# Where the input sums of a seven-product matrix multiplication are formed in a two-layer attention kernel

## The chip, the cores and the metric

The kernel runs on one core of one Trainium2 chip. The metric is device microseconds of one execution. The engines are named as the profile names them: PE is TensorE (matrix products; PEld its weight loads), DVE is VectorE, ACT is ScalarE, POOL is GpSimd and SP is SyncE. [...]

## What is computed

The reference, cut to what matters; there are two such layers, one after the other:

```python
# x: (16, 256, 32, 32); b = 16 images, c = 256 channels, n = 32*32 = 1024 positions
def layer(x, Wq, bq, Wk, bk, Wv, bv, rel_h, rel_w):        # 4 heads of d = 64
    y = _gn(x)                       # (y - mean) / sqrt(var + 1e-5) in 16 groups of the last axis
    xf = y.reshape(b, c, n)
    q, k, v = (einsum('oc,bcn->bon', W, xf) + bias[None, :, None] for W, bias in ...)
    sim  = einsum('bhdi,bhdj->bhij', q, k)
    rel  = (rel_h + rel_w).reshape(heads, d, n)
    qpos = einsum('hdi,bhdj->bhij', rel, q)
    attn = softmax(sim + qpos, axis=-1)
    out  = einsum('bhdn,bhmn->bhdm', v, attn)
    return x + out.reshape(b, c, w, h)
```

All numbers are float32.

## The kernel before

The work is cut into 32 units, one for each image and layer. Their order is written out by hand in the list `units`, so that an image's second layer comes some units after its first. A unit has four blocks, b = 0 to 3: two pairs of heads (`pr`) times two halves of the 1024 query positions (`half`). A block works on a score matrix of both heads of the pair against 8 groups of 128 key positions, j = 0 to 7, each held in a tile of 128x1024 in two PSUM banks. There are four such pairs of banks, and the list `ring` says which of them is used for what.

For each j, `seed` (L447, VectorE) writes the position term into PSUM, `scores` (L483, TensorE) adds the product of q and k, ScalarE takes the exponential into a tile p (L492), and `add_up` (L522, L524, VectorE) adds p to the block's running sum acc. `attend` (L537, TensorE) multiplies the p of all j with the values. The last one or two p of a block are added to acc in the next block, by adding transfers from POOL (`add_last`, L555); a p buffer comes free only when they have landed. The sums over the partitions are folded by more transfers: `fold` (L560, POOL), `stack_up` (L574, SP), `fold_again` (L579, POOL), `fold_stack` (L584, POOL, several times with falling sizes) and `spread_sums` (L592, SP), which writes them into den_all. One and a half units of blocks later `reciprocals` takes 1/den_all on VectorE (L634), writes it to DRAM (rd, L636, SP) and reads it back spread over the partitions (rden, two transfers, L641, SP). `normalise` (L649, VectorE) multiplies the block's output od by it, and `add_by_dma` (L667, POOL) adds that to the image x.

In every block other work stands between the scores: the next unit's projections (`project`, L268; `positions`, L424, which ScalarE copies out at L435), its norm, and its values. The norm of unit u + 2 is computed by sums and squares on ScalarE (L190), a small product on TensorE, and in `norm_var` a reduction on VectorE (L235) followed on POOL by the power -0.5 (L237) and the shift (L239, tile nshift). `norm_apply` (L248, ScalarE) writes the normalised image xn, in pieces spread over blocks 0 and 1.

The order of instructions on each engine is the order in which the code calls them; nothing reorders them. An engine that waits holds all that stands behind it in its own queue.

The values of unit u + 1 are computed in block 3 (`block_with_values`) by the seven-product scheme for a 2x2 block matrix multiplication. The class `Values` has the seven products: numbers 1, 2 and 3 read quarters of xn, and number 3's weights are a mixture; numbers 4, 5, 6 and 7 read t, a tile of four quarters of 128x512 that are sums of quarters of xn. With the quarters called x0 to x3,

- t0 = x1 + x0, t1 = x1 + x3
- t2 = t0 + x3, t3 = t2 + x2

The products go through two banks, in four pairs of stages called "1" to "4", with copies by ScalarE (`keep`, L404) and additions by VectorE (`combine`, L410) between. Stage "2" holds products 6 (which reads t2) and 2 and is the first to read t; "3" reads t0 and t1, "4" reads t3.

Before the change t is formed in block 2 by transfers alone: SP copies x1 twice (`sum_copies`, L327), POOL adds x0 and x3 to the two copies (`sum_additions`, L336), SP copies t0 twice, POOL adds x3 to both, and at block 2's end POOL adds x2 to the last quarter.

Of the kernel before, what the change touches and what calls it, by code (L numbers as in the profile page):

```python
# [13 lines left out]
ALU = mybir.AluOpType  # L14
# [3 lines left out]
P = 128  # L18
HALF = 512
# [33 lines left out]
def fast_path(ctx, tc, sh, x, layers, out, W, den_all, good, flag):  # L53
# [26 lines left out]
    nc = tc.nc  # L80
# [234 lines left out]
    sums_x = {}  # L315

    def quarters_of_x(u):
        return xns[u].rearrange("p c (a n) -> p (c a) n", a=2)

    def sum_copies(u, second):  # L320

        x = quarters_of_x(u)
        if not second:
            sums_x[u] = tpool.tile([P, 4, HALF], F32, tag="t", name=f"t_{u}")
        t = sums_x[u]
        into, of = (t[:, 2:4, :], t[:, 0:1, :]) if second else (t[:, 0:2, :], x[:, 1:2, :])
        nc.sync.dma_start(into, of.to_broadcast([P, 2, HALF]))  # L327

    def sum_additions(u, i):
        x, t = quarters_of_x(u), sums_x[u]  # L330
        into, of = (
            (t[:, 0:2, :], x[:, 0:4:3, :]),
            (t[:, 2:4, :], x[:, 3:4, :].to_broadcast([P, 2, HALF])),
            (t[:, 3, :], x[:, 2, :]),
        )[i]
        nc.gpsimd.dma_start(into, of, accum_op=ALU.add)  # L336

    def by_token(bank):
        return bank.rearrange("p (i c) -> p i c", c=P)
# [102 lines left out]
    def seed(blk, j, tag):  # L442

        u, pr, half = blk
        ps = psum2(tag, f"ps_{u}_{pr}_{half}_{j}")
        ab = abt[u, pr][:, :, j, :]
        nc.vector.tensor_tensor(  # L447
            ps.rearrange("p h (w y) -> p h w y", y=H),
            ab[:, :, :H].unsqueeze(2).to_broadcast([P, 2, XH, H]),
            ab[:, :, H + half * XH : H + (half + 1) * XH]  # L450
            .unsqueeze(3)
            .to_broadcast([P, 2, XH, H]),
            ALU.add,
        )
        seeds[blk, j] = ps
# [60 lines left out]
    def add_up(blk, j):  # L516
        u, pr, half = blk
        if j == 0:
            return
        if j == 1:  # L520
            accs[blk] = apool.tile([P, 2, HALF], F32, tag="acc", name=f"acc_{u}_{pr}_{half}")
            nc.vector.tensor_tensor(accs[blk], probs[blk, 0], probs[blk, 1], ALU.add)  # L522
        else:
            nc.vector.tensor_tensor(accs[blk], accs[blk], probs[blk, j], ALU.add)  # L524
# [102 lines left out]
    def reciprocals(u, pr, count=2):  # L627

        n = index[u, pr, 0]
        r8 = fpool.tile([P, 2, 8], F32, tag="r8", name=f"r8_{u}_{pr}")
        nc.vector.reciprocal(r8[:, :count, :], den_all[:, n : n + count, :])  # L634
        rd = dpool.tile([P, count * 8], F32, tag=f"rd{count}", name=f"rd_{u}_{pr}")
        nc.sync.dma_start(rd, r8[:, :count, :].rearrange("p x e -> p (x e)"))  # L636
        rden = opool.tile([P, 2 * HALF], F32, tag="rden", name=f"rden_{u}_{pr}")
        rdens[u, pr] = rden
        rd = rd.rearrange("(h k) e -> h (k e)", h=2)
        for h, hs in enumerate(QUARTERS):  # L640
            nc.sync.dma_start(  # L641
                rden[hs, : count * HALF],
                rd[h : h + 1].to_broadcast([D, count * HALF]),
            )
# [117 lines left out]
    def block(n):  # L762
        blk = blocks[n]
        u, b = divmod(n, BPU)
        pr_, half = blk[1:]

        stacked = blocks[n - 3][:2] if half == 1 and n > 2 else None
        summed = blocks[n - 4][:2] if half == 0 and n > 3 else None
        last_unit = u + 1 == NU
        before = blocks[n - 5][:2] if b == 1 and n > 4 else None  # L770
        after = blocks[n + 1] if n + 1 < len(blocks) else None
        previous = blocks[n - 1] if n > 0 else None
        one, two = u + 1 < NU, u + 2 < NU

        pieces = u + 1 < NU or b < 2
        if u + 1 == NU and b == 1:
            widen(u, 1)
        f0, f1, f2, f3 = ring
        folded = n - 1 < FOLDED
        if not pieces:  # L780
            return block_without_pieces(n, half)
        if b == 0 and u > 0:
            return block_with_q(n)
        if b == 3:
            return block_with_values(n)

        if b == 2:
            sum_copies(u + 1, False)
        if previous and folded and b == 1:
            add_last(previous, NT - 2)  # L790
        elif previous:
            add_up(previous, 6)
            if folded:
                add_last(previous)
            else:
                add_up(previous, 7)
        for j in range(1 if n > 0 else 2, 4):
            scores(blk, j)
        (first, first_out), (second, second_out) = prepare(u, b)
        first(0)  # L800
        norms(u, b, 0)
        if n == 1:
            reduced(2, 1)
            added(2)
        seed(blk, 4, f1)
        scores(blk, 4)
        add_up(blk, 1)
        if before:
            reciprocals(*before)
        norms(u, b, 1)  # L810
        second(0)
        if half == 1:
            second_out()
        if b == 2:
            sum_additions(u + 1, 0)
            sum_copies(u + 1, True)
        if stacked:
            fold_stack(*stacked, D)
        if summed:
            fold_stack(*summed, R // 8)  # L820
            spread_sums(*summed)
        if previous and folded:
            fold(previous)
        if stacked:
            fold_stack(*stacked, R)
        if b == 2:
            sum_additions(u + 1, 1)
        first(1)
        first_out()
        seed(blk, 5, f0)  # L830
        scores(blk, 5)
        if previous and folded:
            stack_up(previous)
        if b == 2 and n > 5:
            store(*blocks[n - 6][:2])
        add_up(blk, 2)
        if n == 0:
            reduced(2, 0)
        if half == 0:
            second(1)  # L840
            second_out()
        seed(blk, 6, f1)
        scores(blk, 6)
        if half == 0:
            ring[2:] = f3, f2
        seed(blk, 7, ring[2])
        scores(blk, 7)
        add_up(blk, 3)
        add_up(blk, 4)

        if after:
            seed(after, 0, f0)
        if n in check:
            next(checks)
        norms(u, b, 2)
        po = psum2(ring[3], f"po_{n}")
        values_of_p = attend(blk, po)
        values_of_p(0)
        if two and half == 1:
            mean_out = norm_mean(u + 2, filled(f1, f"pm_{n}", 0.0))  # L860
        if after:
            scores(after, 0)
        if n == 0:
            mean_out = norm_var(1, filled(f1, f"pm_{n}", EPS / 2))
        if stacked:
            fold_stack(*stacked, R // 2)
        if previous and folded:
            fold_again(previous)
        if b == 2:
            sum_additions(u + 1, 2)  # L870
        if half == 1 and u + 3 < NU and units[u + 3][1] == 0 and u > 0 or n == 3:
            load_x(units[u + 3][0], range(pr_, pr_ + 1) if u > 0 else range(CC))
        add_up(blk, 5)
        if n in (2, 6):
            W.mix(n // 4)
        if before and last_unit:
            finish(*before)
        elif before:
            normalise(*before)
            add_by_dma(*before)  # L880
        if two and half == 1 or n == 0:
            mean_out()
        if stacked:
            fold_stack(*stacked, R // 4)
            if n == len(blocks) - 3:
                fold_stack(*stacked, R // 8)
                spread_sums(*stacked)
        if after:
            for j in range(1, 4):
                seed(after, j, ring[j % 3])  # L890
        norms(u, b, 3)
        values_of_p(1)
        take_out(blk, po)
        pos[n] = po
# [55 lines left out]
    def block_with_values(n):  # L950

        blk = blocks[n]
        u = blk[0]
# [6 lines left out]
        add_last(previous, NT - 2)  # L960
        scores(blk, 1)
        add_up(blk, 1)
        if before:
            reciprocals(*before)
        one = v.half(1, HI, False), v.half(1, LO, True)
        two_halves = score_half(blk, 2, 0), score_half(blk, 2, 1)
        v.stage("1", (two_halves[0], two_halves[1]), (one[0], one[1]), 0)
# [11 lines left out]
        v.keep(1, 0, 1.0)  # L979
        seed(blk, 5, r2)  # L980
        scores(blk, 5)
        seed(blk, 6, r1)
        scores(blk, 6)
        v.combine(0, 0, ALU.add)
# [24 lines left out]
        scores(after, 0)  # L1009
        v.pair("4", 3, 4, 1)  # L1010
        v.keep(0, 1, -1.0)
        fold_stack(*stacked, R // 2)
        fold_again(previous)
        if u + 3 < NU and units[u + 3][1] == 0:
            load_x(units[u + 3][0], range(1, 2) if u > 0 else range(CC))
        add_up(blk, 4)
        if two:
            mean_out()
        ring[:] = r1, r0, r3, r2
        seed(after, 1, r0)  # L1020
        if before:
# [526 lines left out]
```

## Time and profile before

| | |
|---|---|
| time, median of 3 runs | 2975.96 us (2975.19 to 2991.6) |
| profiled execution | 2993.0 us, span of its instructions 2989.0 us |
| PE busy | 2645.2 us (88%) |
| DVE busy | 2162.0 us (72%) |
| ACT busy | 2014.6 us (67%) |
| POOL busy | 1044.8 us (35%) |
| mean granted clock of TensorE | 0.946 |
| moved by DMA | 375.48 MB |

Busy times are shares of the whole span. Idle time in front of an instruction is shown in the profile beside what released it ("<-"): where TensorE is the engine that sets the pace, its own idle times and their releasers are the lines to read, and the other engines' idle times matter only where TensorE waits for them. The granted clock is the share of full speed at which TensorE was allowed to run. A unit of four blocks takes some 93 us, and most of what the trace shows repeats from unit to unit.

### The profile page before, as it was taken

How to read it: one execution, taken by the hardware profiler on the slowest of the kernel's cores; microseconds unless marked ns; L12 is line 12 of the kernel's file. 1: busy time of each engine (PE TensorE's matmuls, PEld its weight loads, DVE VectorE, ACT ScalarE, POOL GpSimd, SP SyncE). 2: the span in 40 equal slices, each digit the busy share in tenths (PEclk: the TensorE clock that was granted, in tenths of full speed). 3: DMA queues.
4: the chain of work that ended last, by engine and by line, in shares of the span. 5: the costliest groups of instructions: out<-in, count | busy, mean ns of one | idle time of the engine just before them, and what ended most of it. 6: DMA issues, size and time to landing. Idle time of an engine off the chain costs nothing. (4 is left out here: it accounts for less than half of the span.)

```text
span 2989.0 us, 94281 instructions
## 1 busy us (share of the span) xinstructions
PE 2645.2 (88%) x41192; PEld 1458.4 (49%) x41192; DVE 2162.0 (72%) x2091; ACT 2014.6 (67%) x3977; POOL 1044.8 (35%) x1122
## 2 busy tenths in 40 slices
PE   8988989888988889888899888988889888999897
PEld 4555544444445544454545544444454444444453
DVE  7877777666776767767777666776777767777777
ACT  7866776667766667666777666766677666776654
POOL 1334333333333433334343333333433334333330
PEclk9999999999989999999999999999999889999999
DMA  3666665667666666666766666566676556665663
GB/s 103 121 116 130 135 121 107 124 143 143 119 117 145 130 126 121 120 131 131 147 126 130 125 119 133 119 124 131 134 150 132 111 116 127 140 122 105 125 137 87
DMA packets 180099, 375.48 MB, mean 126 GB/s; under 512 B 58840, under 2 KB 60376, under 8 KB 179680
## 3 DMA queue, kind: packets, MB, share of 16 engines
q0 software_dynamic: 97072, 250.97, 48.4%
q1 hardware_dynamic: 82608, 118.41, 13.4%
q8 instruction: 326, 5.34, 0.7%
q14 instruction: 93, 0.76, 0.1%
HBM read 51.78 MB, written 17.30 MB: 23 GB/s over the span
## 5 line engine op out<-in xcount | busy, mean ns | idle before, releaser
L492 ACT ACTIVATE p<-ps,shift 128x1024 f32<-128x1024 f32 x993 | 1069.7, 1112 | 650.0 <-PE ps L483 570.5
L447 DVE TENSOR_TENSOR ps<-abt 128x1024 f32<-128x1024 f32 x1018 | 1225.6, 1227 | 331.2 <-ACT p L492 279.5
L483 PE MATMUL ps<-q,k 64*64 64x512 f32 x7944 | 1029.6, 612 | 100.8 <-DVE ps L447 96.6
L537 PE MATMUL po<-p,v 64*64 64x256 f32 x16384 | 973.5, 386 | 29.2 <-ACT q L279 27.1
L537 PEld LDWEIGHTS po<-p,v 64*64 64x64 f32 x16384 | 650.9, 137 | 377.0 <-issue 79.6
L524 DVE TENSOR_TENSOR acc<-acc,p 128x1024 f32<-128x1024 f32 x550 | 670.0, 1218 | 3.8
L483 PEld LDWEIGHTS ps<-q,k 64*64 64x64 f32 x7944 | 296.2, 137 | 516.5 <-DVE ps L447 249.9
L555 POOL DMA_DIRECT2D acc<-p x217 | 266.3, 1227 | 605.3 <-DMA acc<-p 241.4
L584 POOL DMA_DIRECT2D stack<-stack x310 | 308.8, 996 | 273.4 <-DMA stack<-stack 237.0
L368 PE MATMUL pw<-mixed,t 64*64 64x128 f32 x2976 | 172.7, 306 | 193.5 <-DMA t<-xn 193.5
L579 POOL DMA_DIRECT2D stack<-acc x248 | 215.6, 980 | 325.3 <-DMA stack<-acc 287.0
L248 ACT ACTIVATE xn<-x,nshift,rstd 128x128 f32<-128x128 f32 x496 | 209.1, 493 | 122.2 <-POOL nshift L239 122.2
L368 PEld LDWEIGHTS pw<-mixed,t 64*64 64x64 f32 x2976 | 151.6, 155 | 232.3 <-issue 208.8
L268 PE MATMUL pq<-xn,Wq 64*64 64x512 f32 x2048 | 243.0, 590 | 0.0
L268 PE MATMUL pk<-xn,Wk 64*64 64x512 f32 x2048 | 242.5, 589 | 0.0
L560 POOL DMA_DIRECT2D acc<-acc x124 | 102.0, 823 | 399.9 <-DMA acc<-p 389.5
L410 DVE TENSOR_TENSOR v<-v,pw 128x512 f32<-128x512 f32 x93 | 63.9, 687 | 240.9 <-ACT v L404 240.9
L522 DVE TENSOR_TENSOR acc<-p,p 128x1024 f32<-128x1024 f32 x128 | 156.4, 1222 | 93.9 <-ACT p L492 90.8
L336 POOL DMA_DIRECT2D t<-xn x93 | 130.2, 1400 | 249.3 <-DMA t<-t 195.8
L190 ACT ACTIVATE junk<-x,neg 128x128 f32<-128x128 f32 x505 | 197.7, 399 | 0.0
L368 PE MATMUL pw<-Wv,xn 64*64 64x128 f32 x1984 | 173.1, 326 | 0.2 <-issue 0.2
L368 PEld LDWEIGHTS pw<-Wv,xn 64*64 64x64 f32 x1984 | 148.4, 167 | 45.6 <-issue 45.4
(95 smaller groups left out, 1902.2 us busy)
## 6 DMA issues: line engine op xcount, KB each, us to landing
acc<-p POOLq DMA_DIRECT2D x217, 512.0 KB, 6.7
rden<-rd SPq DMA_DIRECT2D x126, 256.0 KB, 5.3
acc<-acc POOLq DMA_DIRECT2D x124, 256.0 KB, 3.6
t<-xn POOLq DMA_DIRECT2D x62, 512.0 KB, 6.9
x<-od POOLq DMA_DIRECT2D x61, 512.0 KB, 5.2
x<-in_x_dram SPq DMA_DIRECT2D x32, 512.0 KB, 4.3
stack<-acc SPq DMA_DIRECT2D x248, 64.0 KB, 2.1
stack<-acc POOLq DMA_DIRECT2D x248, 64.0 KB, 3.2
```

The lines of the kernel that those rows point to most:

```text
L190: nc.scalar.activation(junk, grouped(xt[units[u][0]], g), func, accum_out=into[:, g : g + 1], **bias)
L248: nc.scalar.activation(grouped(xns[u], g), grouped(xt[units[u][0]], g), AF.Identity, bias=shift[:, g : g + 1], scale=rstd[:, g : g + 1],)
L268: yield nc.tensor.matmul(pk[c, nh, :], w[l][rs, cc, c0 : c0 + D], xns[u][rs, cc, nh * HALF : (nh + 1) * HALF], start=(t == 0 and cc == 0), ...
L368: yield nc.tensor.matmul(self.pw[c, a, part * P : (part + 1) * P], x[rs, j0 : j0 + D], w[rs, :], start=first and not whole and part == 0, ...
L447: nc.vector.tensor_tensor(ps.rearrange("p h (w y) -> p h w y", y=H), ab[:, :, :H].unsqueeze(2).to_broadcast([P, 2, XH, H]), ab[:, :, H + h ...
L483: nc.tensor.matmul(ps[c, h, :], a[hs, j0 : j0 + D], b[hs, columns], start=bool(tag) and i == 0, stop=i == len(terms) - 1, skip_group_check ...
L492: nc.scalar.activation(p, ps, AF.Exp, bias=W.shift)
L524: nc.vector.tensor_tensor(accs[blk], accs[blk], probs[blk, j], ALU.add)
L537: yield nc.tensor.matmul(po[c, a, :QUART], vts[u][rs, pr, j, h * D : (h + 1) * D], p[rs, h, a * QUART : (a + 1) * QUART], start=(t == 0 an ...
L555: nc.gpsimd.dma_start(accs[blk], probs[blk, j], accum_op=ALU.add)
L579: nc.gpsimd.dma_start(at, acc[R:D, h, :], accum_op=ALU.add)
L584: nc.gpsimd.dma_start(stack[:rows_], stack[rows_ : 2 * rows_], accum_op=ALU.add)
```

## The change

t is formed by VectorE in three operations instead of two copies and three adding transfers. The first writes t0 and t1 together, the second t2, the third t3. They are issued in block 2: the first behind the additions of the previous block's last p, the second behind `add_up` 2, the third behind `add_up` 3.

Two other steps change places. `reciprocals` goes, in block 1, from behind `add_up` 1 to behind `add_up` 2, which is one seed and one addition later on VectorE; in block 3 it goes from behind `add_up` 1 to behind the scores of j = 5, two seeds later. And in block 3 `add_up` 4 and `mean_out`, which holds the reduction on VectorE and the power and the shift on POOL, go ahead of `fold_stack` with R // 2, `fold_again` and the load of x.

```diff
-    def sum_copies(u, second):
+    def add_inputs(u, i):
         x = quarters_of_x(u)
-        if not second:
+        if i == 0:
             sums_x[u] = tpool.tile([P, 4, HALF], F32, tag="t", name=f"t_{u}")
         t = sums_x[u]
-        into, of = (t[:, 2:4, :], t[:, 0:1, :]) if second else (t[:, 0:2, :], x[:, 1:2, :])
-        nc.sync.dma_start(into, of.to_broadcast([P, 2, HALF]))
-
-    def sum_additions(u, i):
-        x, t = quarters_of_x(u), sums_x[u]
-        into, of = (
-            (t[:, 0:2, :], x[:, 0:4:3, :]),
-            (t[:, 2:4, :], x[:, 3:4, :].to_broadcast([P, 2, HALF])),
-            (t[:, 3, :], x[:, 2, :]),
+        into, one, other = (
+            (t[:, 0:2, :], x[:, 0:4:3, :], x[:, 1:2, :].to_broadcast([P, 2, HALF])),
+            (t[:, 2, :], t[:, 0, :], x[:, 3, :]),
+            (t[:, 3, :], t[:, 2, :], x[:, 2, :]),
         )[i]
-        nc.gpsimd.dma_start(into, of, accum_op=ALU.add)
+        nc.vector.tensor_tensor(into, one, other, ALU.add)
...
 # block (b = 1 and b = 2)
-        if b == 2:
-            sum_copies(u + 1, False)
...
             else:
                 add_up(previous, 7)
+        if b == 2:
+            add_inputs(u + 1, 0)
...
         add_up(blk, 1)
-        if before:
-            reciprocals(*before)
...
-        if b == 2:
-            sum_additions(u + 1, 0)
-            sum_copies(u + 1, True)
...
-        if b == 2:
-            sum_additions(u + 1, 1)
...
         add_up(blk, 2)
+        if before:
+            reciprocals(*before)
+        if b == 2:
+            add_inputs(u + 1, 1)
...
         add_up(blk, 3)
+        if b == 2:
+            add_inputs(u + 1, 2)
         add_up(blk, 4)
...
-        if b == 2:
-            sum_additions(u + 1, 2)
...
 # block_with_values (b = 3)
         add_up(blk, 1)
-        if before:
-            reciprocals(*before)
...
         seed(blk, 5, r2)
         scores(blk, 5)
+        if before:
+            reciprocals(*before)
...
+        add_up(blk, 4)
+        if two:
+            mean_out()
         fold_stack(*stacked, R // 2)
         fold_again(previous)
         if u + 3 < NU and units[u + 3][1] == 0:
             load_x(units[u + 3][0], range(1, 2) if u > 0 else range(CC))
-        add_up(blk, 4)
-        if two:
-            mean_out()
```

## The prediction

> **What bounds the kernel now.** I read the page's busy shares first, then the list of waits, then TensorE's timeline around its longest wait, then the windows with the granted clock, and last GpSimd's queue.
>
> ```profile
> PE 2645.2 (88%) x41192; PEld 1458.4 (49%) x41192; DVE 2162.0 (72%) x2091; ACT 2014.6 (67%) x3977; POOL 1044.8 (35%) x1122
> ...
> L368 PE MATMUL pw<-mixed,t 64*64 64x128 f32 x2976 | 172.7, 306 | 193.5 <-DMA t<-xn 193.5
> ```
>
> TensorE is the fullest engine, yet idle for 2989.0 - 2645.2 = 344 us. More than half of that, 193.5 us, lies ahead of one group: the products that read the tile t of input sums. The list of waits gives the number of times and the next waits of TensorE:
>
> ```profile
> PE pw L368 <- DMA t<-xn: 193.5, 30, 10.8
> PE ps L483 <- DVE ps L447: 96.6, 67, 5.3
> PE po L537 <- ACT q L279: 27.1, 30, 1.2
> ```
>
> So in 30 of the 31 blocks with values, stage "2" waits 193.5 / 30 = 6.45 us for an adding transfer into t. TensorE's timeline in the unit near 1570 us (us from the start, duration, engine, line, operation, in brackets the idle time before):
>
> ```profile
> 1563.75 1.18 PE L424 MATMUL pa<-rel,q 64*64 64x64 f32 x64
> 1569.93 0.48 PE L368 MATMUL pw<-mixed,t 64*64 64x128 f32 x2 [5.00 <-DMA t<-xn]
> ...
> 1597.39 1.04 PE L483 MATMUL ps<-q,k 64*64 64x512 f32 x8
> 1599.33 1.09 PE L483 MATMUL ps<-q,k 64*64 64x512 f32 x8 [0.90 <-DVE ps L447]
> 1601.62 3.68 PE L537 MATMUL po<-p,v 64*64 64x256 f32 x64 [1.20 <-ACT q L279]
> ```
>
> The products behind the wait take 0.45 to 0.48 us where the same ones take 0.27 us elsewhere. The windows say why (us; busy time and count of PE, PEld, DVE, ACT, POOL; granted clock; DMA share; GB/s):
>
> ```profile
> 1560.00:1565.00 5.00, 4.93 (x156) 3.68 (x146) 1.23 (x1) 3.65 (x7) 0.51 (x1) 1.00 0.49 138
> 1565.00:1570.00 5.00, 0.07 (x4) 0.10 (x7) 3.64 (x4) 1.70 (x2) 2.45 (x3) 0.85 0.91 206
> 1570.00:1575.00 5.00, 5.00 (x72) 3.85 (x76) 0.00 (x0) 1.11 (x1) 1.74 (x2) 0.50 0.99 182
> 1575.00:1580.00 5.00, 4.95 (x101) 3.10 (x97) 3.96 (x4) 3.56 (x4) 1.23 (x2) 0.97 0.56 144
> ```
>
> While TensorE idles the granted clock falls to 0.50, and it stays there for some 5 us of full work. After the shortest wait (1.30 us, at 172.89) it stayed at 1.00.
>
> Last, GpSimd's queue in the same unit:
>
> ```profile
> 1564.49 1.23 POOL L336 DMA_DIRECT2D t<-xn  x1 [6.29 <-DMA t<-t]
> 1567.60 1.73 POOL L579 DMA_DIRECT2D stack<-acc  x2 [1.88 <-DMA stack<-acc]
> 1570.08 0.86 POOL L336 DMA_DIRECT2D t<-xn  x1 [0.74 <-DMA t<-xn]
> 1570.64 1.18 POOL L555 DMA_DIRECT2D acc<-p  x1
> ...
> 1591.93 3.83 POOL L237 TENSOR_TENSOR rstd<-var,mhalf 128x16 f32<-128x16 f32 x1
> ```
>
> The second addition waits 6.29 us for SP's copy and the third comes 0.4 us behind it in queue order; block 3's first add_last (L555) is stuck behind them, and the power (L237) comes 21 us after that. TensorE's small waits at 1599 and 1601 are the power's doing: ScalarE waits for nshift (29 times, 122.2 us in all), its exp is late, VectorE's next seed waits for that exp.
>
> **The change, part by part.** The unit of account is the period from one such wait's end to the next: 29 periods, 2705.97 us, mean 93.3. TensorE is busy 82.4 of it.
>
> *1. The wait of stage "2" goes.* The first sum is issued in block 2 behind add_up of the previous block's p and before seed 4. There VectorE ended add_up at 1540.6 and sat idle 1.94 us until 1542.60, and xn's last ScalarE part ended at 1539.2. The other two stand behind add_up 2 and 3, so t is complete near 1553; stage "2" could start at 1564.9, when positions end. Next due there is bank 0, whose copy (L404) ended at 1564.8, so no other wait takes its place. Gain 193.5.
>
> *2. The half clock behind it goes too.* In the 8 us after each of the 30 landings the granted clock averages 0.731 with TensorE busy 237.63 of 240 us: 240 x 0.269 = 64.6 us. A wait must stay near 1.3 us or less to be sure of this (2.65 us already cost some).
>
> [...]
>
> *3. The power earlier.* mean_out moves past three issues of POOL: one fold_stack and the two DMAs of fold_again; these now queue behind it, and x's load on SP keeps its place. On VectorE its reduction keeps its place too. In the timeline it slips into a gap (POOL waited 3.05 us until 1590.23 there). Also the three L336 leave, so block 3's first add_last can issue at about block start + 1 instead of + 10.3 us (1570.64 against 1560.3). Counted from that issue, the rows give the second add_last at + 8.1, fold at + 13.4, the next fold_stack at + 15.8, then power and shift 4.5 us: nshift at about start + 21. ScalarE needs it at start + 25.4 (block 3 of 21.2 us without the wait, then the 4.2 us it took from block 0's start to the wait). Margin 4 us. What this pays: waits 28 to 36 us after a landing, in block 0, sum to 67.6 (VectorE's seed) + 26.7 (ScalarE's q) us, and the clock there, 26 to 44 us after, falls to 0.81 in ten units and 0.91 in nine: 18 x (10 x 0.19 + 9 x 0.09) = 48.8 us, some 44 of it under work. Together 138; I take 80%, 110, as the margin is an estimate; bounds 0 (nshift still late) and 138.
>
> *4. Three VectorE operations.* They stand where two SP and three POOL transfers did. Nearest rows: 1.22 us for 128x1024 (L524), 0.69 for 128x512 (L410): 1.22 + 2 x 0.69 = 2.6 us per unit, x31 = 81 us of VectorE. The first fits the 1.94 us idle; the others delay seeds 6 and 7 by at most 0.7 and 1.4 us, and block 2's VectorE had 6.7 us idle. If that cover is gone, all 81 us are on the path. Bounds 0 and 81; I take 10, as the shown idle is the nearest row.
>
> *5. Reciprocals later.* In block 1 they move behind seed 5 and add_up 2, in block 3 behind seeds 4 and 5. VectorE waited 115.8 us there for den_all (46 times), with seed 5 behind it; TensorE's waits in block 1 sum to 13.9 us, and this gain I book. Against it: rd and rden (three SP DMAs, in order) start about 2.5 us later, and normalise (L649), behind which the next block's seeds stand, waits for them. Two reciprocals in the rows were followed by rden 9.4 us later at most (1525.31 to 1534.68, no wait) and 11.1 us later (1616.04 to 1627.15, a wait of 1.64). In the new order about 7 to 8 us of VectorE work lie between. So 1 to 3.5 us of wait in block 1, perhaps half of it felt by TensorE, 1.2 us x 31 = 37. SP's queue is freer: L327 held it 428.9 us. Net cost -23; bounds +14 and -95.
>
> *6. Lighter transfers.* Four issues of 512 KB and one of 256 KB go, 2.3 of 375.48 / 31 = 12.1 MB per unit; not on TensorE's path by themselves. 0.
>
> *7. Closer engines.* A unit without its waits is 82.4 - (64.6 + 44) / 30 = 78.8 us of TensorE; VectorE has 66.8 + 2.6 of work (1936.20 us in the 29 periods, and term 4); GpSimd's serial chain of adds and folds is 90 us (rival B) less 7.0 for t's two waits and 4.5 for the power, 78.5. Order-bound waits of about 0.8 us per unit, 25 us; bounds 0 and 100.
>
> [...]
>
> **Sum.** 193.5 + 64.6 + 110 - 10 - 23 - 25 = 310 us. The profiled execution took 2993.0 us (span 2989.0), 0.6% above the median of 2975.96; 2993 - 310 = 2683, and from the median 2976 - 310 = 2666. I take 2665.
>
> **Rivals.**
> A. Only the wait and its clock go, the power's waits stay: 2976 - 193.5 - 64.6 + 58 = 2776 (costs 10 + 23 + 25). For it: ScalarE's wait is spread over 29 units, and the order on GpSimd is a long serial chain. Against it: 9 us of POOL delay go with L336.
> B. GpSimd's chain becomes the bound. Issue distances in the trace between the blocks' first add_last: 27 + 20.7 + 21.4 + 20.8 = 90 us per unit. If they stay, 3.3 us x 30 = 99 us gained: 2877. For it: exp already waits for add_last's buffers (72.6 us, 42 times). Against: the 20.8 and the 27 contain t's waits and the late power.
> C. Slower: normalise. If rden lands more than 8 us later than the 9.4 to 11.1 us above, TensorE stalls about 6 us in blocks 1 and 3, and at half clock loses 2.2 more each: 16.4 against 10.3 gained per unit, x31 = +189: 3165. It decides from about 5 us of stall in each. Nothing in the trace is near it, and the transfers become lighter.
> D. Stage "2" waits for something else due at the same time: 193.5 stays, power's gain 110 against 81 + 23: about 2970. The copy of bank 0 (1564.8 against 1564.9) is the only candidate, and it is on time.
>
> **How the numbers follow.** Forecast 0.66, A 0.17, B 0.12, C 0.03, D 0.02. The forecast's own bounds, 2600 (110 becomes 138, costs 0 and net +14) to 2730; A's place makes the range 2600 to 2790, with B's most part, C and D outside. About 1% is what a measurement of this kernel tells from no change: faster 0.95, same 0.02, slower 0.03.
>
> **What would show it.** Right: no wait of L368 for t in TensorE's list; granted clock above 0.99 in nearly all slices; three VectorE groups near 1.22 and 0.69 us, x31 each; ScalarE's wait for nshift below 30 us; TensorE above 94% busy. Wrong: seeds of the block after normalise waiting on rden for over 3 us, ScalarE's exp waiting on add_last for more than 100 us, or a clock that falls without an idle time before it.

## The result, and the profile after

The changed kernel takes 3067.47 us (median of 4 runs, 3064.96 to 3071.79) against 2983.16 us for the kernel before in the same comparison (4 runs, one more than in the table above): ratio 1.0284, 95% interval 1.0244 to 1.0323. It is slower; the forecast was 2665 us. The profiled execution has a span of 3063.2 us and a mean granted clock of 0.929 (before 0.946).

The page of the changed kernel, its busy shares and the group of products that read t:

```profile
PE 2593.9 (85%) x41192; PEld 1453.6 (47%) x41192; DVE 2229.4 (73%) x2184; ACT 2017.4 (66%) x3977; POOL 969.8 (32%) x1029
...
L644 DVE TENSOR_TENSOR od<-od,rden 128x1024 f32<-128x1024 f32 x63 | 77.6, 1231 | 470.4 <-DMA rden<-rd 470.4
...
L363 PE MATMUL pw<-mixed,t 64*64 64x128 f32 x2976 | 135.6, 271 | 1.8 <-issue 1.8
```

The change did what it says: the products that read t wait for next to nothing (1.8 us, 193.5 before) and run at 271 ns (306 before). But a new line is there: normalise, whose line is L644 now, holds VectorE for 470.4 us until rden lands. Before, this wait was small:

```profile
DVE od L649 <- DMA rden<-rd: 22.2, 13, 2.9
```

The waits of TensorE in the changed kernel show where this ends:

```profile
PE ps L478 <- DVE ps L442: 420.9, 34, 16.3
PE po L532 <- ACT q L279: 15.1, 30, 0.5
```

TensorE's wait for seeds has risen from 96.6 to 420.9 us. It is one long wait per unit, at the start of block 2. Here it is near 1580 us, first on TensorE, then on VectorE:

```profile
1572.44 3.63 PE L532 MATMUL po<-p,v 64*64 64x256 f32 x64
1590.87 4.52 PE L478 MATMUL ps<-q,k 64*64 64x512 f32 x24 [14.79 <-DVE ps L442]
```

```profile
1564.44 0.25 DVE L629 RECIPROCAL r<-den_all 128x16 f32<-128x16 f32 x1
...
1588.13 1.23 DVE L644 TENSOR_TENSOR od<-od,rden 128x1024 f32<-128x1024 f32 x1 [16.50 <-DMA rden<-rd]
1589.27 0.18 DVE L219 TENSOR_REDUCE neg<-pm 128x16 f32<-128x32 f32 x1
1589.49 3.50 DVE L442 TENSOR_TENSOR ps<-abt 128x1024 f32<-128x1024 f32 x3
```

The reciprocal itself waits for nothing and is done at 1564.7. Yet rden lands only 23 us later; VectorE stands at normalise, and the three seeds of block 2 stand behind it. SP's queue says where those 23 us went:

```profile
1579.74 1.11 SPq L569 DMA_DIRECT2D stack<-acc  x2
1580.90 0.58 SPq L631 DMA_DIRECT2D rd<-r  x1
1583.14 1.31 SPq L636 DMA_DIRECT2D rden<-rd  x2
```

rd is issued 16.2 us after its data are ready, right behind stack_up of the previous block (L569). That transfer needs the fold of the previous block to have landed, and GpSimd issued the fold only at 1576.25:

```profile
1576.25 0.81 POOL L555 DMA_DIRECT2D acc<-acc  x1 [2.02 <-DMA acc<-p]
```

In the source, the reciprocals' call moved in block 1 from ahead of `stack_up(previous)` to behind it. On VectorE this is one seed and one addition; on SP the three transfers moved past stack_up.

In the 14.79 us that TensorE idles here the clock falls to 0.50, and the next block starts at half speed: 0.50 from 1590 to 1594, 1.00 again from 1596 (windows of the changed kernel: busy times of PE, PEld, DVE, ACT, POOL; granted clock; DMA share; GB/s):

```profile
1572.00:1580.00 8.00, 4.08 (x72) 2.45 (x64) 0.00 (x0) 3.70 (x8) 2.72 (x4) 1.00 0.70 123
1580.00:1590.00 10.00, 0.00 (x0) 0.00 (x0) 1.84 (x3) 0.00 (x0) 2.83 (x4) 0.54 0.38 84
1590.00:1600.00 10.00, 9.13 (x72) 3.25 (x76) 10.00 (x10) 5.21 (x9) 3.52 (x5) 0.78 0.59 109
```

### The profile page after: what moved, and what is told of

The parts are those of the page before. It is cut to its first block, busy times and chain, and to the rows that moved or that the text cites. A ratio compares the mean times of both kernels' runs of the same rounds, so it can differ in the third digit from the quotient of the medians.

```text
span 3063.2 us, 94037 instructions
## 1 busy us (share of the span) xinstructions
PE 2593.9 (85%) x41192; PEld 1453.6 (47%) x41192; DVE 2229.4 (73%) x2184; ACT 2017.4 (66%) x3977; POOL 969.8 (32%) x1029
## 5 line engine op out<-in xcount | busy, mean ns | idle before, releaser
L478 PE MATMUL ps<-q,k 64*64 64x512 f32 x7944 | 1048.7, 628 | 429.0 <-DVE ps L442 420.9
L532 PE MATMUL po<-p,v 64*64 64x256 f32 x16384 | 943.2, 377 | 15.1 <-ACT q L279 15.1
L478 PEld LDWEIGHTS ps<-q,k 64*64 64x64 f32 x7944 | 316.0, 139 | 854.5 <-issue 658.9
L519 DVE TENSOR_TENSOR acc<-acc,p 128x1024 f32<-128x1024 f32 x550 | 670.9, 1220 | 2.8
L550 POOL DMA_DIRECT2D acc<-p x217 | 226.0, 1042 | 654.0 <-ACT p L487 168.2
L644 DVE TENSOR_TENSOR od<-od,rden 128x1024 f32<-128x1024 f32 x63 | 77.6, 1231 | 470.4 <-DMA rden<-rd 470.4
L237 POOL TENSOR_TENSOR rstd<-var,mhalf 128x16 f32<-128x16 f32 x31 | 122.9, 3964 | 238.3 <-DVE var L235 238.3
L594 ACT COPY od<-po 128x512 f32<-128x512 f32 x127 | 74.4, 586 | 136.6 <-PE po L532 136.6
L268 PEld LDWEIGHTS pq<-xn,Wq 64*64 64x64 f32 x2048 | 82.2, 138 | 151.2 <-issue 142.4
L190 ACT ACTIVATE junk<-x 128x128 f32<-128x128 f32 x464 | 140.2, 313 | 0.0
L363 PE MATMUL pw<-mixed,t 64*64 64x128 f32 x2976 | 135.6, 271 | 1.8 <-issue 1.8
```

Source lines behind the costliest of these rows:

```text
L190: nc.scalar.activation(junk, grouped(xt[units[u][0]], g), func, accum_out=into[:, g : g + 1], **bias)
L268: yield nc.tensor.matmul(pk[c, nh, :], w[l][rs, cc, c0 : c0 + D], xns[u][rs, cc, nh * HALF : (nh + 1) * HALF], start=(t == 0 and cc == 0), ...
L478: nc.tensor.matmul(ps[c, h, :], a[hs, j0 : j0 + D], b[hs, columns], start=bool(tag) and i == 0, stop=i == len(terms) - 1, skip_group_check ...
L532: yield nc.tensor.matmul(po[c, a, :QUART], vts[u][rs, pr, j, h * D : (h + 1) * D], p[rs, h, a * QUART : (a + 1) * QUART], start=(t == 0 an ...
L550: nc.gpsimd.dma_start(accs[blk], probs[blk, j], accum_op=ALU.add)
```

## The experiments

Theory Q: the loss is SP's queue order alone. Theory V: the reciprocals come too late on VectorE itself. Theory W: the three added VectorE operations cost it. All ratios below are to the kernel before, run on the same chip, with 95% intervals.

### The reciprocals of block 1 back

"The fast version" below is this kernel: the changed kernel with one call put back.

```diff
         add_up(blk, 1)
+        if before:
+            reciprocals(*before)
...
         add_up(blk, 2)
-        if before:
-            reciprocals(*before)
```

> The changed kernel with the reciprocals of block 1 back behind add_up 1, so that on SP rd and rden stand ahead of stack_up again, and on VectorE ahead of seed 5. Theory Q (SP's queue: rd waits behind stack_up, which waits for the folds of the block before): normalise's wait for rden, 470.4 us in 30 times, falls below 40 us, TensorE's wait for seeds falls from 420.9 to below 80, and the time falls by 420.9 + 30 x 2.2 of half clock, less some 80 of waits that show up instead: 2600 to 2690. Theory W (three more operations on VectorE are the cost): they are still there, so the time stays above 2980.

Measured: 2668.77 us, ratio 0.8985 (0.8951 to 0.902), clock 0.997 in the profiled execution. The busy shares and two waits:

```profile
PE 2551.4 (96%) x41192; PEld 1419.9 (53%) x41192; DVE 2230.3 (84%) x2184; ACT 2017.2 (76%) x3977; POOL 950.7 (36%) x1029
```

```profile
PE ps L478 <- DVE ps L442: 59.0, 74, 2.8
```

```profile
DVE od L644 <- DMA rden<-rd: 43.9, 34, 3.3
```

TensorE waits 420.9 - 59.0 = 362 us less for seeds, and the same 41192 products take 2593.9 - 2551.4 = 42.5 us less as the clock hardly falls any more (mean 0.997 against 0.929): 404 of the 407 us between the spans (3063.2 and 2656.1). Normalise's wait stays a little above the 40 us expected. The added operations are still there, so W falls. Q and V both allow this.

### Only SP's order changed

Against the changed kernel:

```diff
-        if previous and folded:
+        if previous and folded and not before:
             stack_up(previous)
...
         add_up(blk, 2)
         if before:
             reciprocals(*before)
+            if previous and folded:
+                stack_up(previous)
```

> The changed kernel with one thing else: in block 1 stack_up of the previous block is issued behind the reciprocals' three transfers instead of ahead of them. VectorE's order is that of the changed kernel to the last instruction. Theory Q: the same 2600 to 2690 as with the reciprocals back, normalise's wait below 60 us. Theory V (the reciprocals come too late on VectorE itself, one seed and one addition): nothing gained, 3030 to 3070, and normalise still waits over 400 us.

Measured: 2673.62 us, ratio 0.9000 (0.8965 to 0.9035). VectorE's order is the changed kernel's; the loss is gone. The two waits:

```profile
DVE od L644 <- DMA rden<-rd: 90.5, 45, 4.7
PE ps L478 <- DVE ps L442: 60.9, 61, 3.0
```

Normalise still waits 90.5 us in 45 times, more than the 60 expected, but TensorE waits only 60.9 us for seeds. V falls: the later place on VectorE costs nothing that can be measured.

### The reverse: VectorE's order kept, SP's transfers late

Against the fast version; with `later=True`, `reciprocals` does the division only and returns its three transfers (rd, rden, rden), to be issued by `transfers()`:

```diff
         add_up(blk, 1)
         if before:
-            reciprocals(*before)
+            transfers = reciprocals(*before, later=True)
...
             stack_up(previous)
+        if before:
+            transfers()
```

> The fast version (reciprocals of block 1 back behind add_up 1) with VectorE's order untouched, but rd and rden issued on SP behind stack_up of the previous block. Theory Q (SP's queue order alone makes the loss): the whole loss is back, normalise waits for rden over 400 us, 3030 to 3090. Theory V (the place on VectorE): 2660 to 2690 as the version it is made from.

Measured: 3070.41 us, ratio 1.0287 (1.0263 to 1.0311), the changed kernel's to within the interval. The two waits (normalise is L649 here):

```profile
DVE od L649 <- DMA rden<-rd: 468.3, 30, 18.5
PE ps L478 <- DVE ps L442: 420.2, 36, 16.7
```

With the run before it, this settles the cause from both sides: with VectorE's order left as it is, the order of stack_up and the three transfers on SP takes the whole loss away or brings it back.

### The move of block 1 by itself

The kernel before, with only this (lines of before):

```diff
         add_up(blk, 1)
-        if before:
-            reciprocals(*before)
...
         add_up(blk, 2)
+        if before:
+            reciprocals(*before)
```

> The kernel before with only the reciprocals of block 1 moved behind add_up 2, hence behind stack_up on SP. Theory Q: a wait of normalise for rden of 10 to 18 us per unit appears; TensorE loses most of it and half-clock time; the stage-2 wait for t stays or shrinks a little as its transfers get time. 3200 to 3450. Theory V: the move delays the reciprocal by 2.5 us on VectorE, so some 37 us at most: 2960 to 3020. Theory W: no change.

Measured: 3154.44 us, ratio 1.0613 (1.0572 to 1.0653), below the 3200 expected. VectorE's wait for rden and TensorE's for seeds:

```profile
DVE od L649 <- DMA rden<-rd: 532.5, 30, 20.7
PE ps L483 <- DVE ps L447: 487.2, 36, 19.0
```

The reason that it is not more stands in the group of products that read t, in this run:

```profile
L368 PE MATMUL pw<-mixed,t 64*64 64x128 f32 x2976 | 139.6, 272 | 5.3 <-issue 5.2
```

Their 193.5 us of wait are gone, though t still comes by transfers; the expectation had them stay or shrink a little. ScalarE's wait for nshift shrinks too, from 122.2 to 24.2 us, with the power at its old place. A reading that no run tests by itself: TensorE's long wait at block 2's start gives the queues time, and when stage "2" comes t is there. In any case the waits do not add: against the kernel before, TensorE waits 487.2 - 96.6 = 391 us more for seeds and 193.5 us less for t, and is busy 45 us less (2600.1 us), 152 of the 165 us between the spans (3154.2 and 2989.0). This run and the changed kernel differ by the sums, the power's place and block 3's reciprocals, and by 0.033 in the ratio (1.0613 against 1.0284), some 98 us. Most of that is the stall itself: TensorE waits 487.2 us for seeds here and 420.9 us there. The sums and the power, worth 232 and 62 to 67 us in the runs below, are worth little beside this stall.

### The input sums alone

The kernel before with `add_inputs` in place of copies and adding transfers; reciprocals and power at their old places.

```diff
-            sum_copies(u + 1, False)
...
+            add_inputs(u + 1, 0)
...
-            sum_additions(u + 1, 0)
-            sum_copies(u + 1, True)
...
-            sum_additions(u + 1, 1)
...
+            add_inputs(u + 1, 1)
...
+            add_inputs(u + 1, 2)
...
-            sum_additions(u + 1, 2)
```

> The kernel before with only the input sums on VectorE; reciprocals and power where they were. Theory Q, with the steps 1, 2, 4 of the prediction: 193.5 + 64.6 gone, 10 to 40 lost, part of the power's 138 us also gone as POOL's queue is freer: 2640 to 2770, and no wait of the products for t. Theory W: 2980 or more.

Measured: 2743.39 us, ratio 0.9221 (0.9182 to 0.926), clock 0.983 in the profiled execution. By the ratio 0.0779 x 2976 = 232 us. Steps 1, 2 and 4 of the prediction together said 193.5 + 64.6 - 10 = 248. The products no longer wait for t, and TensorE is busy 2584.1 us against 2645.2 before. ScalarE still waits 107.2 us for nshift, 122.2 before, so the freed queue of GpSimd brought little of the power's gain, where the expectation had a part of it.

### The sums written twice

Against the fast version:

```diff
-        nc.vector.tensor_tensor(into, one, other, ALU.add)
+        for _ in range(2):
+            nc.vector.tensor_tensor(into, one, other, ALU.add)
```

> The fast version with each of the three sums on VectorE written twice (the same values): another 2.6 us per unit, 81 us in all, of VectorE. If block 2's idle time hides such work, as step 4 says (10 us felt), the time is 2670 to 2700. If VectorE is on the path in block 2, up to 2750.

Measured: 2672.80 us, ratio 0.8950 (0.8921 to 0.8979) against 0.8985 for the fast version. VectorE is 2306.4 - 2230.3 = 76 us busier and nothing is lost that can be measured. TensorE's wait for seeds is 77.4 us against 59.0, so some of it may be felt, but it is below what the ratios can tell. That block 2's idle time hides the rest is the reading of step 4; no run tests it by itself.

### The power's place, in the fast version and in the kernel before

The same edit in both directions: in the fast version `add_up(blk, 4)` and `mean_out()` of block 3 go back behind `fold_again` and the load; in the kernel before they are moved ahead of `fold_stack(*stacked, R // 2)`. The diff is that of the fast version's run:

```diff
-        add_up(blk, 4)
-        if two:
-            mean_out()
         fold_stack(*stacked, R // 2)
         fold_again(previous)
...
+        add_up(blk, 4)
+        if two:
+            mean_out()
```

> The fast version with mean_out in block 3 back behind fold_again, so that the power is late on POOL again. By step 3 of the prediction (power's move is worth some 110 us): ScalarE's wait for nshift is back at about 107 us as in the run with the sums alone, and the time is 2730 to 2770. If POOL's freed queue already did most of it, the two differ by less than 30 us, 2670 to 2700, and the difference between the sums alone and the fast version is that of block 3's reciprocals.

Measured: 2743.79 us, ratio 0.9194 (0.9164 to 0.9225): 0.0209 x 2976 = 62 us lost against the fast version. ScalarE's wait for nshift, which had gone in the fast version, is back. The line of the kernel before and the line of this run:

```profile
ACT xn L248 <- POOL nshift L239: 122.2, 29, 7.2
...
ACT xn L248 <- POOL nshift L239: 107.4, 28, 5.8
```

> The kernel before with only block 3's mean_out moved ahead of fold_stack R // 2 and fold_again. The sums still come by transfers, so POOL is still late by some 10 us in block 3. If the power's gain does not need the sums' change: ScalarE's wait for nshift falls from 122 to below 40 us and the time by 50 to 110 us, 2870 to 2930. If it needs POOL's freed queue: less than 30 us gained, 2950 to 2990.

Measured: 2912.84 us, ratio 0.9776 (0.976 to 0.9791): 67 us gained. ScalarE's wait for nshift falls to 7.7 us, TensorE's wait for seeds is 46.6 us (96.6 before), and its wait for t is untouched (194.3 us). So the move does not need GpSimd's queue freed of the sums, which step 3 of the prediction had taken as part of the reason.

### Block 3's reciprocals, and two other places

In the fast version, block 3's reciprocals go back too:

```diff
         add_up(blk, 1)
+        if before:
+            reciprocals(*before)
...
         scores(blk, 5)
-        if before:
-            reciprocals(*before)
```

> The fast version with block 3's reciprocals back behind add_up 1 as well, so that none of the reciprocals' moves is left. In block 3 stack_up comes behind them in either place on SP, so no queue is passed: theory Q says no loss and no large gain from that move, within 25 us of 2669.

Measured: 2667.09 us, ratio 0.8955 (0.8912 to 0.8999). No difference from the fast version that can be measured. In block 3 stack_up stands behind the reciprocals at either place, so their transfers pass nothing that waits.

Then block 1's reciprocals at a third place (against the changed kernel):

```diff
         scores(blk, 5)
+        if before:
+            reciprocals(*before)
         if previous and folded:
             stack_up(previous)
...
         add_up(blk, 2)
-        if before:
-            reciprocals(*before)
```

> The changed kernel with block 1's reciprocals behind the scores of j = 5 and directly ahead of stack_up: on VectorE still behind seed 5, on SP ahead of stack_up again. Theory Q: fast, 2640 to 2680; against the fast version it saves the part of the wait for den_all (33.0 us in 24 times) that TensorE felt, and pays as normalise's wait grows: within 20 us of it either way. Theory V: slow, 3050.

Measured: 2662.90 us, ratio 0.8957 (0.893 to 0.8983). VectorE waits 11.0 us for den_all (33.0 in the fast version) and 59.5 us for rden (43.9); the two nearly cancel. The fast version, this one and the one above cannot be told apart, and each takes about 10% less than the kernel before.

Last, the fast version with block 1's normalise behind the next seeds:

```diff
-        elif before:
-            normalise(*before)
-            add_by_dma(*before)
...
             for j in range(1, 4):
                 seed(after, j, ring[j % 3])
+        if before and not last_unit:
+            normalise(*before)
+            add_by_dma(*before)
```

> The fast version with block 1's normalise (and add_by_dma) behind the next block's seeds 1 to 3 instead of ahead of them. If the rest of normalise's wait (43.9 us in 34 times) is felt by TensorE, 2635 to 2660; if its place was already free of cost, the same 2669 within 10 us. If the later add_by_dma on POOL holds up add_last, 2680 to 2700.

Measured: 2691.45 us, ratio 0.9023 (0.8999 to 0.9047). Its interval overlaps the fast version's, so no loss against it is shown, and no gain; against the run above (0.8957) it is slower by 0.007. ScalarE's wait for add_last's buffers is 107.8 us here against 74.1 in the fast version, which would fit the third expectation. But the two runs above lose nothing with 94.2 and 100.1 us of it, so this does not show the cause, which stays open.

## Why the prediction was wrong

The step that failed is 5. It said "rd and rden (three SP DMAs, in order) start about 2.5 us later" and "SP's queue is freer", and booked -23 us with bounds of +14 and -95. Measured, from the ratios of the changed kernel and the fast version: (1.0284 - 0.8985) x 2976 = 387 us. In the unit shown rd was issued 16.2 us after its data were ready, and the order on SP alone takes the loss away (ratio 0.9000) or brings it back (1.0287). The 2.5 us were counted on VectorE. The move's three transfers go into SP's queue, and what stood between their old and their new place there was not listed. The trace of before had it, in the same unit from which step 5 took its 11.1 us:

```profile
1617.05 0.40 SPq L636 DMA_DIRECT2D rd<-r  x1
1619.64 1.12 SPq L641 DMA_DIRECT2D rden<-rd  x2
1635.81 1.13 SPq L574 DMA_DIRECT2D stack<-acc  x2
```

The next issue on SP after the reciprocals' own is block 1's stack_up, 16 us later, and the list of SP's waits, from which step 5 took L327's 428.9 us, has at its top what it stands for:

```profile
SPq L574 <- DMA acc<-acc: 860.8, 89, 38.7
```

Whatever is moved behind that line is issued after 1636.9 instead of at 1617. From rd's issue to rden's landing it takes 7 us (1580.90 to 1588.13, after) to 10 us (1617.05 to 1627.15, before); VectorE was at normalise at 1625.5, so it would wait 19 to 22 us, an estimate from this one unit. The move by itself gave 532.5 / 30 = 17.8 us. So the stall, which makes the result, could be read to within some microseconds from the trace of before, where the 10 us stand.

Rival C named the place (normalise waiting for rden, TensorE at half clock behind it, 0.50 in the unit shown) but with the wrong price and chance: 6 us in each of two blocks, 0.03, "Nothing in the trace is near it". TensorE lost 420.9 / 30 = 14 us in one block. The prediction's first sign of being wrong, seeds behind a wait for rden of over 3 us, is what came; of its signs of being right, the waits for t and nshift did go.

The other steps, each measured by its own run:

- Steps 1, 2 and 4, the sums: 248 forecast, 232 measured. That doubled sums cost nothing that can be measured bears out step 4; if anything its 10 us were too many.
- Step 2, the half clock: 64.6 us forecast; in the run with the sums alone the products are busy 2645.2 - 2584.1 = 61 us less. With the power moved too, in the fast version, it is 2551.4 us, 94 us less for the same instructions, 3.1% of the span before, where steps 2 and 3 had 64.6 + 44. Behind 29 of the 30 waits for t in the kernel before the clock averages 0.62 to 0.83 in the next 8 us; behind the shortest, of 1.30 us, it stays at 1.00. A wait of 2.65 us was long enough: the one that ended at 2691.22 was followed by a clock of 0.50 from 2691.5 to 2694.
- Step 3, the power: 110 forecast, 62 and 67 measured. The wait for nshift did go, so the direction is right and the size was too large.
- The sum: without step 5 the terms come to 333 us; the fast version gained (1 - 0.8985) x 2976 = 302. The sums were booked 16 us too high and the power some 45, together 61, which is more than the 31 us missing. The rest is step 7's cost of 25 us, for which the runs leave no room that can be seen: the sums alone and the power alone, 232 and 62 to 67, already add up to the fast version's gain. That 2665 was forecast for the changed kernel and the fast version took 2668.77 is chance: gains booked too high met costs, in steps 5 and 7, that the fast version does not show.
- The power beside VectorE's work: in the fast version it runs in block 3 beside additions, and these take no longer for it. The longest of the 550 additions (L519) took 1241 ns at a median of 1218. The power at 1412.92 took 3.34 us with a whole addition inside it (1414.93, 1.22 us); the one in the kernel before that ran beside no VectorE work, at 199.19, took 3.25 us. All 31 took 3.21 to 4.39 us in the fast version and 3.25 to 4.53 us in the kernel before.

## What to carry to other kernels

A call that is moved takes its transfers along: for each queue on which it issues, write out what stands between the old place and the new one, and when each of these can go. Here a transfer that waited for data from elsewhere was a gate for what was put behind it, however short the move looked on the computing engine: behind stack_up rd was issued 16.2 us after its own data were ready. And two stalls in one period need not add: beside the new stall, the old wait of 193.5 us for t was gone with t's transfers unchanged. So a true gain can stay unseen until the new stall is taken away.

## What the runs showed that was not expected

- The idle stretch of 14.79 us in the unit shown cost TensorE more than its length: the clock was 0.54 in the last 10 us of it or so, and 0.78 in the 10 us after. Over the run the same products were busy 42.5 us longer than in the fast version.
- VectorE had room for 76 us more work in block 2 at no cost that can be measured, although it was already busy 84% of the span and TensorE 96%.
- With the reciprocals of block 1 late and nothing else changed, two waits of the kernel before went or shrank by themselves: TensorE's for t (193.5 us) and ScalarE's for nshift (122.2 to 24.2 us).
